# Staged first loads, first sums strip by strip, and output halves at the end of a two-layer LoRA kernel

## The chip, the cores and the metric

The kernel runs on one core of a Trainium2 chip. The metric is device time in microseconds of one execution; lower is better. The core has five engines that each work through their own instruction queue in program order: TensorE (PE; its weight loads are a row of their own, PEld), VectorE (DVE), ScalarE (ACT), GpSimd (POOL), and SyncE (SP), which here only issues DMAs. POOL issues the gathers (indirect DMAs). An instruction that waits holds up everything behind it on its engine.

## The reference

Two residual LoRA layers over x (64 requests of 64 tokens, 1024 channels, fp32), one after the other:

```python
x = x + _L0_cond_ref(x, L0_cond_A, L0_cond_B, itok_B_4_50)
#   Bx = x @ B[id].T ; out = Bx @ A[id].T       one adapter of rank 16 per request
x = x + _L1_cond_ref(x, itok_B_0_7, L1_cond_W, L1_cond_Wr, L1_cond_A, L1_cond_B)
#   base = x @ W.T
#   logits = x @ Wr.T + 5 * one_hot(language id)   8 experts, the top 2, softmax of the two
#   lora = sum over experts of gate * (x @ A[e].T) @ B[e].T
#   out = base + 2 * lora
```

## The kernel before

x is held transposed (channels on the partitions) in 8 blocks of 512 tokens. A block is two tiles of 1 MB, `("x", k, 0)` and `("x", k, 1)`, with 4 chunks of 128 channels each; a strip of a tile is 128 tokens of it. Block k goes through two phases. The first, `early(k)`, is layer 0:

- `gather` fetches the rows of B (tile gb) and of A (tile ga) of the block's 8 requests from HBM, 512 KB each, by an indirect DMA on POOL.
- `turn` transposes gb on PE (tile pt), 4 chunks at a time, and ACT copies it out (tile bt).
- `project` multiplies bt by all 8 chunks of x into one PSUM tile (the pb with 128x128 outputs, 64 instructions), and DVE masks it to bx.
- `adapt` multiplies ga by bx, one half of the channels at a time (tile px), and DVE adds the result to x, one strip of one half at a time: 8 sums a block.

The second phase, `late(k)`, is the routing part of layer 1: `rows` multiplies each strip of x by A and Wr of layer 1 (tiles ph; the two operands lie side by side in a1_sb, whose last columns POOL copies from wr_c), `gates` works out the gates on DVE, `weigh` transposes the gated rows on PE (pg). A strip of `rows` needs the sums of both halves of that strip.

The base product x @ W.T, with the identity added to W's diagonal blocks (`add_identity`, DVE) for the residual, is done for two blocks at a time with a two-level Strassen scheme of 7 outer products, in the order 1, 2, 6, 7, 5, 3, 4; each has 7 inner products numbered likewise (`step(n, k)`), and the last two inner products of each outer one are put off and interleaved with the next. The very first outer product is done directly (`whole_product`, tile pw). `leave` adds a PSUM result to the outputs on DVE, `done` stores a finished output tile (512 KB). For the first pair the sums of weights are made on POOL and kept in HBM; later pairs load them back.

No order of instructions is written by hand. Each step is put into a `Plan` with its engine and an assumed duration, what it reads and writes, an urgency `at` (lower is earlier), and kb for a DMA's size. `Plan.order` simulates the engines with these durations, takes at each point the most urgent step that can start within 0.2 us of the earliest, and the program is issued in the order of the simulated starts. What an instruction really waits for is added afterwards from the tiles that it touches. The assumed numbers therefore decide only the order in each queue. LAG is the assumed hand-over between engines, LAND and KB the landing and rate of a DMA, GATHER the extra time of a gather, SET the time at which an engine is free at the beginning.

What touches the change, by lines: `add` 57, `order` 64, `consts` 308, `load` 353, `gather` 367, `turn` 379, `project` 400, `adapt` 428, `gates` 504, `load_w` 597, `add_identity` 606, `products` 777 with `done` 892 and `step` 940. Every instruction is recorded through one helper, so the profile calls them all L29; they are told apart by the tiles. The beginning is set up by these lines (988 to 997):

```python
    consts()
    for k, at in ((0, -58), (1, -42)):
        for i in range(2):
            load(k, i, at)
        gather(k, "gb", b0, at - 1)
        gather(k, "ga", a0, at)
    ...
            load_w(q0[0] + i, q0[1] + j, at)
    early(0, -40)
```

In the program before, SP's queue begins with the ids of layer 0, both halves of block 0, wr_c, the language ids (ids1_sb), A of layer 1, four tiles of W, both halves of block 1, and the other twelve tiles of W. POOL's begins with the gathers gb and ga of block 0, gb and ga of block 1, the copy of wr_c into a1_sb, and then gb of block 2 and so on, as their two buffers come free.

Of the kernel before, what the change touches and what calls it, by code (L numbers as in the profile page):

```python
# [14 lines left out]
P = 128  # L15
# [18 lines left out]
class Plan:  # L34
# [8 lines left out]

    LAG = 0.3
    LOOK = 0.2
    LAND = 2.2
    KB = 350.0
    GATHER = 4.0
    AHEAD = 6.0
    PACE = {"DVE": 0.4, "POOL": 0.75}  # L50
    SET = {"SP": 1.2, "DVE": 3.1, "POOL": 3.6}

# [3 lines left out]

    def add(self, eng, fn, reads=(), writes=(), at=0.0, take=(), kb=0, sb=False):

        self.steps.append(
            dict(n=len(self.steps), eng=eng, fn=fn, reads=list(reads), writes=list(writes),  # L60
                 at=at, take=list(take), kb=kb, sb=sb)
        )

    def order(self):
        steps = self.steps
        wrote, read, users, tag_of, turns = {}, {}, {}, {}, {}
        for st in steps:
            n, dep = st["n"], set()
            for k in st["reads"]:
                dep.update(wrote.get(k, ()))  # L70
            for k in st["writes"]:
                dep.update(wrote.get(k, ()))
                dep.update(read.get(k, ()))
            for k in st["reads"]:
                read.setdefault(k, []).append(n)
            for k in st["writes"]:
                wrote[k], read[k] = [n], []
            for tag, tile_ in st["take"]:
                tag_of[tile_] = tag
                turns.setdefault(tag, []).append(n)  # L80
            for k in st["reads"] + st["writes"]:
                users.setdefault(k[0], set()).add(n)
            dep.discard(n)
            st["dep"] = dep
        held = [[] for _ in steps]
        left, last = {}, {}
# [5 lines left out]
        for st in steps:  # L92
            for d in st["dep"]:
                after[d].append(st["n"])
        needs = [len(st["dep"]) for st in steps]
        ready = {st["n"] for st in steps if not st["dep"]}
        free = {tag: [0.0] * c for tag, c in self.slots.items()}
# [8 lines left out]
        def start(n, e):  # L106
            st = steps[n]
            t = clock.get(e, 0.0)
            if st["kb"] and e == "SP":
                t = max(t, moved - self.AHEAD)  # L110
            for d in st["dep"]:
                t = max(t, end[d] + (0.0 if where[d] == e and not steps[d]["kb"] else self.LAG))
# [65 lines left out]
def kernel(  # L178
# [129 lines left out]
    def consts():  # L308
# [3 lines left out]
            [], [("ids1",)], -53, kb=32,  # L312
        )
        plan.add({"SP": 0.4}, lambda e: sp.dma_start(a1_sb[:, :, :P], a1), [], [("a1",)], -45, kb=512)
        plan.add({"SP": 0.4}, lambda e: sp.dma_start(b1_sb, b1), [], [("b1",)], -29, kb=512)

        def spread(e):
            pool.tensor_copy(a1_sb[:, :, P:], wr_c)

        def languages(e):  # L320
            per = P // SEQ
# [15 lines left out]

        plan.add({"POOL": 0.3}, spread, [("wr_c",)], [("wr",)], -45)
        plan.add({"DVE": 1.0}, languages, [("ids1",)], [("bias",)], -45)


# [11 lines left out]
    def load(k, i, at):  # L353
        t = ("x", k, i)

        def fn(e):
            made[t] = new("q", [P, HC, TB], f"x_{k}_{i}")
            sp.dma_start(
                made[t],
                xT[i * HC * P : (i + 1) * HC * P, k * TB : (k + 1) * TB].rearrange(  # L360
                    "(c p) t -> p c t", p=P
                ),
            )

        plan.add({"SP": 0.5}, fn, [], part(t), at, [("q", t)], kb=1024)

    def gather(k, tag, table, at):
        def fn(e):
            made[tag, k] = new(tag, [P, D], f"{tag}_{k}")
            pool.indirect_dma_start(  # L370
                out=made[tag, k],
                out_offset=None,
                in_=table,
                in_offset=bass.IndirectOffsetOnAxis(ap=idx[:, k : k + 1], axis=0),
            )

        plan.add({"POOL": 1.1}, fn, [], [((tag, k),)], at, [(tag, (tag, k))], kb=512)

    def turn(k, g, at):
# [11 lines left out]
        def out(e):  # L391
            act.copy(made[bt][:, g * PER : (g + 1) * PER, :], made[pt])

        plan.add(
            {"PE": 0.65}, fn, [(("gb", k),)] + [(bt, 0)] * g, [(pt,)] + [(bt, 0)] * (g == 0), at,
            [("l", pt)] + [("bt", bt)] * (g == 0),
# [3 lines left out]
    def project(k, at):  # L400

        pb, bx = ("pb", k), ("bx", k)

        def fn(e):
            made[pb] = new("l", [P, GT], f"pb_{k}")
            made[bx] = new("bx", [P, GT], f"bx_{k}")
            for c in range(NC):
                for gi in range(NG):
# [10 lines left out]
        def out(e):  # L419
            dve.tensor_tensor(made[bx], made[pb], mask, ALU.mult)  # L420

        plan.add(
            {"PE": 2.2}, fn, [(("bt", k), 1), (("bt", k), 2)] + whole(k), [(pb,), (bx,)], at,
            [("l", pb), ("bx", bx)],
        )
        plan.add({"DVE": 0.3}, out, [(pb,)], [(bx,)], at - 8)

    def adapt(k, h, at):
# [22 lines left out]
        def out(gi):  # L451
# [6 lines left out]
        plan.add(  # L458
            {"PE": 1.4}, fn, [(("ga", k),), (("bx", k),)], [(t,) for t in px], at,
            list(zip(tags, px)),  # L460
        )
        for gi in range(NG):
            xs = part(x, gs=[gi])
            plan.add({"DVE": 0.7}, out(gi), [(px[gi],)] + xs, xs, at - 2)

    def rows(k, at):
# [3 lines left out]
        def strip(j):  # L470
# [14 lines left out]
            def out(e):  # L485
# [5 lines left out]
            plan.add(  # L491
                {"PE": 1.92}, fn, [("a1",), ("wr",)] + xs, [(ph,)], at + j,
                [("l", ph)] * (j % 2 == 0),
# [10 lines left out]
    def gates(k, at):  # L504
# [51 lines left out]
        plan.add({"DVE": 0.9}, lambda e: first(e, 1), [(sm, 1)], [(sm, 2)], at, sb=True)  # L556
        plan.add({"DVE": 0.7}, second, [(sm, 2)], [(sm, 3)], at)
        plan.add({"ACT": 0.25}, exp, [(sm, 3)], [(sm, 4)], at)
        plan.add({"DVE": 0.9}, lambda e: first(e, 2), [(sm, 3)], [(sm, 5)], at, sb=True)
        plan.add({"DVE": 0.8}, share, [(sm, 4)], [(sm, 6)], at, sb=True)  # L560
        plan.add({"DVE": 0.6}, weights, [(sm, 5), (sm, 6)], [(sm, 7)], at, sb=True)
        plan.add({"DVE": 0.7}, gated, [(sm, 7), (h, 0), (h, 1)], [(h, 0), (h, 1)], at, sb=True)

    def weigh(k, at):
# [9 lines left out]
        def out(e):  # L574
            act.copy(made[hg], made[pg].rearrange("p j t -> p (j t)"))

        plan.add(
            {"PE": 0.5}, fn, [(h, 0), (h, 1)], [(pg,), (hg,)], at, [("l", pg), ("hg", hg)]
        )
# [17 lines left out]
    def load_w(i, j, at):  # L597
# [5 lines left out]

        plan.add({"SP": 0.4}, fn, [], [(t,)], at, [("s", t)], kb=256)

    def add_identity(i, at):
# [7 lines left out]

        plan.add({"DVE": 0.5}, fn, [(t,), (("bx", 0),)], [(t,)], at, sb=True)

# [18 lines left out]

    DVE = {"DVE": 0.7}
    POOL = {"POOL": 1.3}

# [115 lines left out]
    def gate_sum(s, n, hd, at):  # L754
# [9 lines left out]
        if n != 3:  # L764
            plan.add({"DVE": 0.42}, fn, [(h,)], [(d,)], at, [("hd", d)], sb=True)
        hd[n] = {
# [10 lines left out]
    def products(s):  # L777
# [24 lines left out]
        ALL = (0, 1)  # L802

        def whole_product(n, i, c):

# [18 lines left out]
            if oh is not None:  # L824
                reads += [("b1",), (whole_h[n],)]
            plan.add(
                {"PE": 3.45 + 0.87 * (oh is not None)}, fn, reads, [(ps,)], at(), [(tag, ps)]
            )
# [4 lines left out]
        def product(n, ps, k, start):  # L833
            last = hd[n][k] if n in (2, 3, 7, 4) and k in (2, 3, 7, 4) else None
            sw, (tx, tk) = wt[n][k], ti[n][k]
# [3 lines left out]
            def fn(e):  # L839
# [3 lines left out]
                for j in range(QC):  # L843
                    mm = [(made[sw][:, c, j * P : (j + 1) * P], tx()[:, c]) for c in range(QC)]
                    if last is not None:
                        o = (oh * 2 + row) * QC + j
                        mm.append((b1_sb[:, o * P : (o + 1) * P], last[0]()))
                    for c, (lhs, rhs) in enumerate(mm):
# [9 lines left out]

            reads = [(sw,)] + tk + ([("b1",), last[1]] if last is not None else [])
            plan.add(  # L860
                {"PE": 1.75 + 0.87 * (last is not None)}, fn, reads, [(ps,)], at(),
                [("a" if k == 1 else "b", ps)] * start,
# [29 lines left out]
        def done(n, i, cs, js):  # L892
# [14 lines left out]
            if oh is None:  # L907
                return
            left[n, i] = left.get((n, i), 2) - 1
            if left[n, i] == 0:  # L910
                o0 = (oh * 2 + i) * QO

# [27 lines left out]
        def step(n, k):  # L940
            i, j = {1: (0, 0), 2: (0, 0), 6: (1, 0), 7: (1, 1), 5: (1, 1), 3: (0, 1), 4: (1, 0)}[k]
            if k in (1, 6, 5, 3):
                ps = ("pa", s, n)
                product(n, ps, k, k == 1)
                leave(n, ps, i, ALL, (j,))
                if k == 5:
                    leave(n, ("pb2", s, n), 1, ALL, (1,), True)
# [3 lines left out]
            else:  # L951
                product(n, ("pb2", s, n), k, k == 7)
                if k == 4:
                    leave(n, ("pb2", s, n), 1, ALL, (0,), True)
# [7 lines left out]
        for n in ORDER:  # L962
# [20 lines left out]
            step(n, 5)  # L983
            rest = [(n, 3), (n, 4)]
        for k in rest:
            step(*k)

    consts()
    for k, at in ((0, -58), (1, -42)):
        for i in range(2):  # L990
            load(k, i, at)
        gather(k, "gb", b0, at - 1)
        gather(k, "ga", a0, at)
    for q0, at in (((0, 0), -43), ((0, 2), -39), ((2, 0), -37), ((2, 2), -36)):
        for i, j in ((0, 0), (1, 0), (1, 1), (0, 1)):
            load_w(q0[0] + i, q0[1] + j, at)
    early(0, -40)
    for i in range(4):
        add_identity(i, -30)
# [73 lines left out]
```

## Time and profile before

| what | us |
|---|---|
| median of three runs (lowest, highest) | 527.1 (525.8, 527.23) |
| the profiled execution's own time | 525.91 |
| its span, first to last instruction | 524.1 |
| PE busy, PEld busy | 504.3, 439.6 |
| DVE, POOL, ACT busy | 294.0, 167.7, 41.1 |
| gathers gb and ga of block 0, issue to landing | 7.6, 7.9 |
| a_sb (A of layer 1) and ids1_sb, issue to landing | 14.7, 13.0 |

The span and the execution's own time differ by 1.8 us, which lies around the span. In the timeline and the page a line reads: line, engine, operation, the tile written and the tiles read, shape, count, then busy time and the mean of one, and in the last column the engine's idle time just before and what ended it. One fp32 matmul shows as two instructions. The clock granted to TensorE was 0.998 of full speed over the span.

### The profile page before, as it was taken

The numbers are of one execution on the slowest core, as the hardware profiler recorded it, in microseconds if no ns is written. First come the engines' busy times: TensorE is split into PE (matmuls) and PEld (weight loads), VectorE is DVE, ScalarE is ACT, GpSimd is POOL, SyncE is SP. The second block draws the span as 40 slices with busy tenths as digits, with TensorE's granted clock in tenths as the row PEclk, the third lists the DMA queues.
The fourth block names the chain that finished last, engine by engine and source line by source line (L and its number), as shares of the span: only waits on it lengthen the run. The fifth ranks groups of instructions, "written<-read, shape, count | busy, mean of one in ns | idle before, by whom it ended". The sixth has DMA issues, their size and how long they took to land.

```text
span 524.1 us, 8532 instructions
## 1 busy us (share of the span) xinstructions
PE 504.3 (96%) x3432; PEld 439.6 (84%) x3432; DVE 294.0 (56%) x572; ACT 41.1 (8%) x81; POOL 167.7 (32%) x139
## 2 busy tenths in 40 slices
PE   1799999999999999999999999999999999999995
PEld 1657988889888988898888998889888898888884
DVE  0679997987974273616674255435476417433632
ACT  1111010001000100012000100001200010001000
POOL 3180068091323144123234313312332323433200
PEclk9999999999999999999999999999999999999999
DMA  8999346689666249726566436844546623710222
GB/s 289 361 362 399 141 147 244 235 298 351 214 220 216 65 141 340 252 73 202 174 204 206 161 100 208 280 138 145 160 155 194 210 84 105 217 41 0 81 80 80
DMA packets 53687, 99.19 MB, mean 189 GB/s; under 512 B 4880, under 2 KB 10000, under 8 KB 53648
## 3 DMA queue, kind: packets, MB, share of 16 engines
q1 hardware_dynamic: 51344, 90.26, 51.8%
q0 software_dynamic: 2304, 8.39, 4.5%
q8 instruction: 27, 0.44, 0.3%
q14 instruction: 12, 0.10, 0.0%
HBM read 69.01 MB, written 29.62 MB: 188 GB/s over the span
## 4 chain that ended last, share of the span: by engine, by line
PE 95%; DMA 2%; DVE 1%; issue 0%; SPq 0%
PE pa L29 39%; PE pb L29 37%; PE ph L29 11%; PE px L29 3%; PE pw L29 3%; DMA ids_sb<-in_ids 2%; PE pt L29 1%; PE pg L29 1%; SPq L29 0%; DVE o L29 0%; DVE bias L29 0%; DVE lang L29 0%; DVE bx L29 0%
## 5 line engine op out<-in xcount | busy, mean ns | idle before, releaser
L29 PE MATMUL pa<-ti,s 128*128 128x256 f32 x432 | 102.5, 381 | 0.0
L29 PE MATMUL pb<-ti,s 128*128 128x256 f32 x384 | 95.7, 380 | 0.0
L29 PEld LDWEIGHTS pa<-ti,s 128*128 128x128 f32 x432 | 80.7, 190 | 11.2 <-issue 0.2
L29 PEld LDWEIGHTS pb<-ti,s 128*128 128x128 f32 x384 | 72.2, 190 | 10.0 <-POOL s L29 0.2
L29 PEld LDWEIGHTS ph<-a_sb,x 128*128 128x128 f32 x512 | 62.7, 190 | 3.3 <-issue 2.2
L29 PE MATMUL ph<-a_sb,x 128*128 128x136 f32 x512 | 63.3, 279 | 2.0 <-issue 2.0
L29 POOL TENSOR_TENSOR ti<-x,ti 128x512 f32<-128x512 f32 x24 | 30.9, 1288 | 78.8 <-PE pb L29 77.9
L29 DVE TENSOR_TENSOR o<-pb,o 128x512 f32<-128x512 f32 x48 | 33.1, 690 | 34.3 <-PE pb L29 20.8
L29 PE MATMUL pa<-x,s 128*128 128x256 f32 x216 | 52.0, 380 | 0.0
L29 POOL TENSOR_TENSOR ti<-t,ti 128x512 f32<-128x512 f32 x18 | 25.2, 1400 | 71.9 <-PE pb L29 54.8
L29 POOL TENSOR_TENSOR ti<-x 128x512 f32<-128x512 f32 x24 | 30.5, 1270 | 52.0 <-PE pb L29 35.9
L29 PEld LDWEIGHTS pa<-x,s 128*128 128x128 f32 x216 | 40.1, 190 | 5.2
L29 DVE TENSOR_TENSOR x<-px,x 128x512 f32<-128x512 f32 x64 | 39.8, 682 | 8.0 <-POOL ti L29 4.3
L29 PE MATMUL pa<-t,s 128*128 128x256 f32 x168 | 41.1, 381 | 0.8 <-DVE o L29 0.8
L29 POOL TENSOR_TENSOR ti<-t 128x512 f32<-128x512 f32 x18 | 24.4, 1353 | 43.4 <-PE pb L29 33.9
L29 DVE TENSOR_TENSOR o<-pa,u 128x512 f32<-128x512 f32 x32 | 22.1, 690 | 26.1 <-PE pa L29 24.8
L29 PEld LDWEIGHTS pa<-t,s 128*128 128x128 f32 x168 | 31.5, 190 | 5.7 <-DVE o L29 1.2
L29 DVE TENSOR_TENSOR u<-pb,u 128x512 f32<-128x512 f32 x21 | 14.5, 690 | 25.6 <-ACT u L29 20.7
L29 PE MATMUL pb<-hg,b_sb 128*128 128x256 f32 x96 | 28.5, 379 | 0.0
L29 DVE TENSOR_TENSOR o<-pa,v 128x512 f32<-128x512 f32 x16 | 11.0, 690 | 26.1 <-PE pa L29 25.8
L29 DVE TENSOR_TENSOR v<-pa,u 128x512 f32<-128x512 f32 x16 | 11.0, 689 | 24.4 <-PE pa L29 24.4
L29 PE MATMUL pb<-x,s 128*128 128x256 f32 x96 | 23.9, 381 | 0.0
(109 smaller groups left out, 592.8 us busy)
## 6 DMA issues: line engine op xcount, KB each, us to landing
s<-s_kept SPq DMA_DIRECT2D x147, 256.0 KB, 2.7
x<-in_xT SPq DMA_DIRECT2D x16, 1024.0 KB, 6.2
out_T<-o SPq DMA_DIRECT2D x32, 512.0 KB, 3.1
s_kept<-s SPq DMA_DIRECT2D x28, 256.0 KB, 3.8
s_kept<-w SPq DMA_DIRECT2D x18, 256.0 KB, 5.1
w<-in_w SPq DMA_DIRECT2D x16, 256.0 KB, 10.1
s_kept<-m SPq DMA_DIRECT2D x3, 256.0 KB, 5.1
a_sb<-in_a SPq DMA_DIRECT2D x1, 512.0 KB, 14.7
```

Of the source, the lines that this page charges most:

```text
L29: return self._tc.keep_in_program_order(f(*args, **kwargs))
```

## The change

The diff does five things. (1) The first x tile is loaded in two DMAs of 512 KB. (2) Some early DMAs are held back by a data dependency: a copy of one column on POOL, from the tile that has to land first into the tile that is to be loaded next, so that the next load waits for POOL and POOL for the first load. The second half of block 0 is so held by the first half of ("x",0,0), and A of layer 1 by gb of block 0. The new argument `behind` asks the planner alone to place a step after another has begun; it adds no wait of its own. (3) DVE's sums of block 0 get urgencies that go by strip; the biases of the language ids and the identity of W are to follow all of block 0's sums (`whole(0)`); `project` is planned as two halves. (4) In the last outer product of the last pair the inner products 4 and 3 change places, the shared PSUM result of product 7 is added to the output before product 5 is done, and the output tiles are stored in halves of 256 KB. (5) The planner's durations are changed.

```diff
-    LAG = 0.3
+    LAG = 0.2
-    LAND = 2.2
+    LAND = 1.8
-    GATHER = 4.0
+    GATHER = 1.5
-    PACE = {"DVE": 0.4, "POOL": 0.75}
-    SET = {"SP": 1.2, "DVE": 3.1, "POOL": 3.6}
+    PACE = {"DVE": 0.36, "POOL": 0.73}
+    SET = {"SP": 1.2, "DVE": 3.1, "POOL": 2.9}
...
+            st["begun"] = {d for k in st["behind"] for d in wrote.get(k, ())} - dep
...
+            for d in st["begun"]:
+                t = max(t, steps[d]["start"] + 0.1)
...
+        def hold(e):
+            pool.tensor_copy(a1_sb[:, 0, :1], made["gb", 0][:, :1])
+        plan.add({"POOL": 0.2}, hold, [(("gb", 0),)], [("a1",)], -56)
         plan.add({"SP": 0.4}, lambda e: sp.dma_start(a1_sb[:, :, :P], a1), [], [("a1",)], -45, kb=512)
-        plan.add({"SP": 0.4}, lambda e: sp.dma_start(b1_sb, b1), [], [("b1",)], -29, kb=512)
+        plan.add({"SP": 0.4}, lambda e: sp.dma_start(b1_sb, b1), [], [("b1",)], -29, kb=512, behind=[("a1",)])
...
-        plan.add({"DVE": 1.0}, languages, [("ids1",)], [("bias",)], -45)
+        plan.add({"DVE": 1.0}, languages, [("ids1",)] + whole(0), [("bias",)], -45)
...
+        held = (k, i) == (0, 1)
+        def hold(e):
             made[t] = new("q", [P, HC, TB], f"x_{k}_{i}")
+            pool.tensor_copy(made[t][:, 0, :1], made["x", 0, 0][:, 0, :1])
+        cuts = ((0, HC // 2), (HC // 2, HC)) if (k, i) == (0, 0) else ((0, HC),)
...
+        if held:
+            plan.add({"POOL": 0.2}, hold, part(("x", 0, 0), [0]), part(t), at, [("q", t)])
+        for c0, c1 in cuts:
+            plan.add(
+                {"SP": 0.5}, lambda e, c0=c0, c1=c1: fn(c0, c1),
+                [], part(t, range(c0, c1)), at, [("q", t)] * (not held and c0 == 0),
+                kb=256 * (c1 - c0), behind=[("a1",)] * (k == 1) + [(t, 0, 0)] * (c0 > 0),
+            )
...
-        plan.add({"POOL": 1.1}, fn, [], [((tag, k),)], at, [(tag, (tag, k))], kb=512)
+        plan.add(
+            {"POOL": 1.1}, fn, [], [((tag, k),)], at, [(tag, (tag, k))], kb=512,
+            behind=[(("x", 0, 1), 0, 0)] * ((tag, k) == ("ga", 0)) + [("a1",)] * (k == 1) + [(("px", 1, 1, 0),)] * (k > 1),
+        )
...
-            {"PE": 2.2}, fn, [(("bt", k), 1), (("bt", k), 2)] + whole(k), [(pb,), (bx,)], at,
+        for h in range(2):
+                {"PE": 0.94}, lambda e, h=h: fn(range(h * HC, (h + 1) * HC)),
+                [(("bt", k), 1), (("bt", k), 2)] + part(("x", k, h)), [(pb,)] + [(bx,)] * (1 - h),
+                at + 0.1 * h, [("l", pb), ("bx", bx)] * (1 - h),
...
-            plan.add({"DVE": 0.7}, out(gi), [(px[gi],)] + xs, xs, at - 2)
+            plan.add({"DVE": 0.62}, out(gi), [(px[gi],)] + xs, xs, at - 2 + 1.5 * gi * (k == 0))
...
-        plan.add({"SP": 0.4}, fn, [], [(t,)], at, [("s", t)], kb=256)
+        plan.add({"SP": 0.4}, fn, [], [(t,)], at, [("s", t)], kb=256, behind=[("a1",)])
...
-        plan.add({"DVE": 0.5}, fn, [(t,), (("bx", 0),)], [(t,)], at, sb=True)
+        plan.add({"DVE": 0.5}, fn, [(t,)] + whole(0), [(t,)], at, sb=True)
...
+            if last(n):
+                def half(e):
+                    t0 = k * TB + js[0] * HT
+                    sp.dma_start(
+                        outT[o0 : o0 + QO, t0 : t0 + HT].rearrange("(c p) t -> p c t", p=P),
+                        q(n, i, ALL, js),
+                    )
+                plan.add({"SP": 0.1}, half, qk(n, i, ALL, js), [], at() + 2, kb=256)
+                return
...
-                leave(n, ps, i, ALL, (j,))
-                if k == 5:
+                leave(n, ps, i, ALL, (j,), k == 5 and last(n))
+                if k == 5 and not last(n):
                     leave(n, ("pb2", s, n), 1, ALL, (1,), True)
...
+                if k == 7 and last(n):
+                    leave(n, ("pb2", s, n), 1, ALL, (1,))
...
-            rest = [(n, 3), (n, 4)]
+            rest = [(n, 4), (n, 3)] if last(n) else [(n, 3), (n, 4)]
...
-    consts()
-    for k, at in ((0, -58), (1, -42)):
-        for i in range(2):
-            load(k, i, at)
+    for k, at in ((0, -60), (1, -42)):
+        load(k, 0, at)
         gather(k, "gb", b0, at - 1)
+        load(k, 1, at)
         gather(k, "ga", a0, at)
+        if k == 0:
+            consts()
     for q0, at in (((0, 0), -43), ((0, 2), -39), ((2, 0), -37), ((2, 2), -36)):
-        for i, j in ((0, 0), (1, 0), (1, 1), (0, 1)):
-            load_w(q0[0] + i, q0[1] + j, at)
+        for i, j in ((0, 0), (0, 1), (1, 0), (1, 1)):
+            load_w(q0[0] + i, q0[1] + j, at + 2 * i * (at == -43))
```

Left out are the steps' other planned durations, each lowered by some hundredths to tenths of a microsecond (a turn from 0.65 to 0.44, a DVE sum from 0.7 to 0.62, a POOL sum from 1.3 to 1.25, an adapt from 1.4 to 1.1).

## The prediction

> **What bounds the kernel now.** I read the page's first part, then its chain of waits, then PE's waits, then the timeline of the first 30 and the last 20 us.
>
> ```profile
> PE 504.3 (96%) x3432; PEld 439.6 (84%) x3432; DVE 294.0 (56%) x572; ACT 41.1 (8%) x81; POOL 167.7 (32%) x139
> PE 95%; DMA 2%; DVE 1%; issue 0%; SPq 0%
> PE pt L29 <- DMA gb<-in_b,idx: 10.6, 1, 10.6
> PE ph L29 <- issue: 2.0, 1, 2.0
> PE px L29 <- DVE bx L29: 1.6, 1, 1.6
> PE pa L29 <- DVE o L29: 0.8, 1, 0.8
> ```
>
> PE is idle for only 524.1 - 504.3 = 19.8 us. The four waits are 15.0 of these; the other 4.8 lie between PE's last product and the end of the span. Between 21.3 and 513 us PE never stops. The change takes no product away, so all that it can win lies in these 19.8 us, and all that it can lose is a new hole in the full stretch. The beginning:
>
> ```profile
> 10.65 1.94 PE L29 MATMUL pt<-ident,gb 128*128 128x128 f32 x8 [10.65 <-DMA gb<-in_b,idx]
> 12.51 2.51 PE L29 MATMUL pb<-x,bt 128*32 128x128 f32 x64
> 14.96 0.66 PE L29 MATMUL pt<-ident,gb 128*128 128x128 f32 x4
> 15.78 0.36 DVE L29 TENSOR_SCALAR lang<-ids_sb 64x32 f32<-64x32 int32 x2 [12.90 <-DMA ids_sb<-in_ids]
> 16.85 0.28 DVE L29 TENSOR_TENSOR bx<-pb,mask 128x128 f32<-128x128 f32 x1
> 17.19 2.07 PE L29 MATMUL px<-bx,ga 32*128 32x128 f32 x64 [1.57 <-DVE bx L29]
> 18.87 0.49 DVE L29 TENSOR_TENSOR w<-w,ident 128x128 f32<-128x128 f32 x2 [1.74 <-DMA w<-in_w]
> 19.28 4.87 DVE L29 TENSOR_TENSOR x<-px,x 128x512 f32<-128x512 f32 x8
> 21.26 3.94 PE L29 MATMUL ph<-a_sb,x 128*128 128x136 f32 x32 [2.01 <-issue]
> ```
>
> Three things delay the first ph. gb lands at 10.5. The product pb is over at about 15.0, yet bx comes at 16.85, because DVE stands at lang, whose ids (32 KB) took 13.0 us to land. The first sum waits behind the identity, which waits for a tile of W. All three are one cause: everything was issued at once and shares the DMA engines. The windows view gives about 400 GB/s from 4 us on, and 1.1 MB moved by 6 us, while 3.1 MB of x and gathers for block 0, 2.1 MB of gathers for blocks 1 to 3, and W were in line by 26 us.
>
> The end:
>
> ```profile
> 513.09 0.69 DVE L29 TENSOR_TENSOR o<-pa,v 128x512 f32<-128x512 f32 x1 [3.62 <-PE pa L29]
> 513.82 0.69 DVE L29 TENSOR_TENSOR o<-pb,o 128x512 f32<-128x512 f32 x1
> 513.84 1.13 PE L29 MATMUL pa<-t,s 128*128 128x256 f32 x4 [0.78 <-DVE o L29]
> 519.32 0.69 DVE L29 TENSOR_TENSOR o<-pb,o 128x512 f32<-128x512 f32 x1 [1.90 <-PE pb L29]
> out_T<-o SPq DMA_DIRECT2D x1, 512.0 KB, 2.8
> ```
>
> Product 3 writes the PSUM tile that DVE is still reading from product 5. After the last sum (over at 520.0) a 512 KB store takes 2.8 us to land.
>
> **Beginning, step by step.** I follow the first ph, since PE is full from there on.
>
> 1. First half of ("x",0,0). The whole tile, issued at 1.19, landed 5.7 later, at 6.9; its 1.05 MB had passed by 5.9, so landing trails the last byte by 1.0. Half of it has passed at 4.55: landed at 5.5. POOL, which has issued gb (2.89 to 4.0) and stands idle, copies the column (0.23, the row of the a_sb copy) by 5.8; SP issues ("x",0,1) at 5.9, its bytes following about 0.9 later.
> 2. gb. Ahead of or beside it now lie 1.05 MB of x and 0.06 of small loads, with its own 0.52: 1.64 MB, passed at 4.55 + 1.12/0.4 = 7.3, landed at **8.2**. Gathers elsewhere in the trace took 4.0 with little beside them, 7.6 here: bounds 6.9 and 10.5. I take 8.2, as the queue is half as long.
> 3. pt at 8.3; from pt to pb it was 1.86 before, so the first half of pb runs from 10.1 to 11.4 (half of 2.51).
> 4. ("x",0,1) and ga together are 1.57 MB from 7.3 on: passed by 11.2, landed by 12.2. Alone, the tile would land at 10.9; with gb of block 1 and A of layer 1 taking 0.5 MB before it, at 13.5. I take **12.3**, later than the 11.5 of before (9.8 after an issue at 1.7): this is what staging costs. ga was issued at 4.3, and comes behind the copy at about 6; it lands by 12 and is needed at 14.
> 5. Second half of pb 12.3 to 13.6, bx and hand-overs 0.5 (at 45 us bx follows pb by 0.15; px followed bx by 0.34): px at 14.1 instead of 17.19. The lang and bias steps (1.1 us) and the identity now follow the sums. There DVE had 2.7 us idle before the gates, which hides them; without that cover they would delay the gates by up to 1.1, not PE.
> 6. First sum 1.3 after px starts (47.22 to 48.53 in block 1): 15.4. By strips, ph needs one sum of each half; the second half's px is over at 16.2, its sum at 16.9, so ph starts at **17.2**. A of layer 1 is issued behind gb, at 8.5, queues behind ("x",0,1), and lands at 13.5 to 15.3: in time, but next in line to be late.
>
> 21.26 - 17.2 = **4.1 us**. Before, half of the transposes of block 1 (0.44 for 4) lay in a PE hole, at 14.96. Now gb of block 1 goes behind the A hold on POOL and lands at about 14; the hole between px and ph (16.2 to 17.2) can take 0.4 to 0.9 of them. Nothing gained or lost, bounds -0.4 and +0.4.
>
> What is queued behind the two holds? On POOL ga, both gathers of block 1 and the wr_c copy (all treated above); on SP, behind A, block 1's x and all W. W's first tiles then land at about 17.5 and are needed at 25 (pw was 7.9 after ph); block 1's x lands near 23, needed at 39. In exchange 1.57 MB of gathers for blocks 2 and 3, issued at 13.7, 19.6 and 25.9 before (first used at 69), are planned later: W should be complete some 4 us earlier than before, when it landed at 39 to 40 and DVE waited for it twice (0.53, 0.43).
>
> **The two rules.** The Trainium skill's page "DMA: Bandwidth & Descriptors", section Bandwidth, tells one to batch DMAs to 1 MiB or more and fits a DMA as 2.0 us plus its bytes at 436 GB/s. Taken one after another, two halves of 512 KB would then cost 6.4 us against 4.4: 2.0 lost. The row speaks otherwise: W's 256 KB loads, queued twelve deep, ran at 350 to 377 GB/s from 30 to 40 us, so the fixed part overlaps; I count nothing for the cut. For the last store, where nothing overlaps, rule and row both count: below. The page "TensorE: Matmul & The Clock Gate", Part 1, says that the array runs at half clock until about 3.4 us of sustained work. An earlier start with holes (11.4 to 12.3, 13.6 to 14.1) may keep it cold through px: up to 2.1 us more. The granted clock shows 1.00 there, but pb took 2.51 at the start against 1.9 later, so something is slow early on; px, after a 1.6 us hole, took 2.07, hardly more than the 2 x 1.1 of block 1. I take the row: none.
>
> **End.** Product 4 comes first and uses the PSUM tile that was emptied after product 7, so the 0.78 goes; DVE's sum of product 5 (0.69) is over before product 3 needs its tile 2.6 us later. The last store is 256 KB: the 512 KB were moved at 385 GB/s in some 1.3 us, half of that is 0.65; the median 256 KB load took 2.7, which would save 0.1. The store is the nearer row: 0.5. Together **1.3 us**.
>
> **The full stretch.** 17 to 110 us is where DVE is dense: 22.7 busy of 24 between 40 and 64 us. Its inputs (gates behind ph, W behind the DMAs, sums behind px) all move by about 4 us with PE, and PE had no wait there, so I count no hole; bounds 0 and 4. Later DVE is at 53% (207 of 390). The planner's lower durations match what one sees (0.61 from sum to sum, 1.23 for POOL alone), so its order need not be worse.
>
> Sum: 4.1 + 1.3 = **5.4 us**. The profiled execution took 525.91; less 5.4 is 520.5. The median of the runs is 1.2 above it, which would give 521.7. I forecast **521.5**.
>
> **Rivals.** A measurement here tells a change from none at about 0.3%, 1.6 us.
>
> - *Given back* (0.16): PE reaches DVE's dense stretch 4 us early and waits there for the sums of block 1 or the t tiles. For: DVE's 95% between 40 and 64. Against: those sums' own inputs come earlier too, and DVE's waits for W go. It leaves the end's 1.3 and a little: 525.
> - *All of it* (0.11): x gets the larger share of the DMA engines, ("x",0,1) lands at 11, ph starts at 15.9 and both transposes of block 1 are hidden: 1.3 + 0.4 more, 519.8. Against: before, that tile got only about half the rate while the gathers ran.
> - *The hold changes nothing for gb* (within the forecast): gb still lands at 10.5. Then pb is over at 15.0, bx and px follow at once (15.5), ph at 18.6: DVE's new order alone gives 2.7, with the end 4.0: 523.
> - *Slower* (0.07): the order is frozen with a gather assumed to land 4.4 us after its start (1.1 + 1.5 + 1.8), where loaded ones took 7.3 to 9.8. A gather for which PE's transposes are queued too early then stops PE by 3 to 5 us. It decides from two such stalls on, once they pass the 5.4; two of 4 us make 529.5. Against: gb of later blocks was issued long before its use (25.9 for use at 69), and only block 1's is near.
>
> The chances: forecast 0.66, all 0.11, given back 0.16, slower 0.07. Faster by over 0.3%: 0.66 + 0.11 + 0.10 (the better part of given back) = 0.87; within 0.06; slower 0.07. Forecast's own bounds are 519.9 to 523.5; the range runs from 519.4, below "all", to 524.8, taking in much of "given back".
>
> **What would show it.** In the changed profile: pt released by gb at 8 to 8.5; no lang before bx; ph near 17.2 with a PE wait before it under 1.2; no PE wait on DVE o at the end, the last store 256 KB landing in 2.3; PE busy still 504, waits between 20 and 500 us near zero. Wrong if gb lands after 10, if A or ("x",0,1) lands after 15, or if PE waits appear between 25 and 110.

## The result

| | before | changed |
|---|---|---|
| median of six runs (lowest, highest), us | 526.98 (525.34, 527.23) | 521.72 (521.31, 522.09) |
| profiled execution's own time, its span | 525.91, 524.1 | 521.59, 519.8 |
| ratio to before, 95% interval | | 0.9914 (0.9899 to 0.9929) |

The change makes the kernel 0.9% faster; 521.5 was forecast. The first line of the changed kernel's page, then PE's waits in it from the view of who waited for whom (total us, times, longest):

```profile
PE 504.9 (97%) x3432; PEld 439.3 (85%) x3432; DVE 300.9 (58%) x572; ACT 41.1 (8%) x81; POOL 170.0 (33%) x141
```

```profile
PE pt L29 <- DMA gb<-in_b,idx: 9.7, 1, 9.7
PE pb L29 <- DMA x<-in_xT: 0.6, 1, 0.6
PE px L29 <- DVE bx L29: 0.4, 1, 0.4
PE ph L29 <- issue: 0.2, 1, 0.2
```

Idle time on PE up to the first ph is 10.9 us instead of 14.2, the wait on DVE at the end is gone, and no wait has come in between 19 and 515 us. The beginning in the timeline, the lines of PE and POOL that answer to those of before:

```profile
4.58 0.18 POOL L29 COPY x<-x 128x1 f32<-128x1 f32 x1 [0.58 <-DMA x<-in_xT]
9.64 0.18 POOL L29 COPY a_sb<-gb 128x1 f32<-128x1 f32 x1 [2.95 <-DMA gb<-in_b,idx]
9.72 1.94 PE L29 MATMUL pt<-ident,gb 128*128 128x128 f32 x8 [9.72 <-DMA gb<-in_b,idx]
11.59 1.54 PE L29 MATMUL pb<-x,bt 128*32 128x128 f32 x32
13.72 1.08 PE L29 MATMUL pb<-x,bt 128*32 128x128 f32 x32 [0.59 <-DMA x<-in_xT]
15.20 2.07 PE L29 MATMUL px<-bx,ga 32*128 32x128 f32 x64 [0.40 <-DVE bx L29]
16.45 4.88 DVE L29 TENSOR_TENSOR x<-px,x 128x512 f32<-128x512 f32 x8 [1.30 <-PE px L29]
17.20 1.25 PE L29 MATMUL pt<-ident,gb 128*128 128x128 f32 x8
18.64 7.65 PE L29 MATMUL ph<-a_sb,x 128*128 128x136 f32 x64 [0.19 <-issue]
```

The two copies are the holds. gb lands at 9.6, the second x tile at 13.6. Nothing stands before bx on DVE; all of block 1's transposes (x8) fit between px and ph. The first ph starts at 18.64 instead of 21.26. The end:

```profile
513.22 0.69 DVE L29 TENSOR_TENSOR o<-pb,o 128x512 f32<-128x512 f32 x1 [1.90 <-PE pb L29]
515.81 0.69 DVE L29 TENSOR_TENSOR o<-pa,v 128x512 f32<-128x512 f32 x1 [1.90 <-PE pa L29]
```

From PE's last product, where this last sum starts, to the end of the span it is 519.8 - 515.8 = 4.0 us; before it was 4.8.

One thing the first profile didn't tell shows in the many runs of the kernel before that were taken beside the experiments: its times lie in two groups, 525.0 to 526.3 and 526.9 to 528.1, about half in each. The changed kernel has one group, 521.2 to 522.1 in twelve runs. The profile of before (525.91) comes from the lower group, so its span tells of a 4.3 us gain where the medians tell of 5.3.

### The profile page after: what moved, and what is told of

Its sections match the earlier page's. It is cut to its first block, busy times and chain, and to the rows that moved or that the text cites. A ratio compares the mean times of both kernels' runs of the same rounds, so it can differ in the third digit from the quotient of the medians.

```text
span 519.8 us, 8542 instructions
## 1 busy us (share of the span) xinstructions
PE 504.9 (97%) x3432; PEld 439.3 (85%) x3432; DVE 300.9 (58%) x572; ACT 41.1 (8%) x81; POOL 170.0 (33%) x141
## 4 chain that ended last, share of the span: by engine, by line
PE 96%; DMA 2%; DVE 0%; issue 0%; SPq 0%; POOL 0%
PE pa L29 39%; PE pb L29 38%; PE ph L29 11%; PE px L29 3%; PE pw L29 3%; DMA x<-in_xT 2%; PE pt L29 1%; PE pg L29 1%; DVE o L29 0%; SPq L29 0%; DVE bx L29 0%; POOL x L29 0%
## 5 line engine op out<-in xcount | busy, mean ns | idle before, releaser
L29 POOL TENSOR_TENSOR ti<-x,ti 128x512 f32<-128x512 f32 x24 | 32.2, 1340 | 78.0 <-PE pb L29 77.1
L29 DVE TENSOR_TENSOR u<-pb,u 128x512 f32<-128x512 f32 x21 | 14.5, 689 | 25.1 <-ACT u L29 20.7
L29 POOL TENSOR_TENSOR s<-w,w 128x512 f32<-128x512 f32 x12 | 17.0, 1418 | 36.0 <-DVE w L29 36.0
```

Of the source, the lines that this page charges most:

```text
L29: return self._tc.keep_in_program_order(f(*args, **kwargs))
```

## The experiments

Twelve kernels, one of them the changed one again; of three only one execution was timed. "First ph" is the point from which PE is full; the kernel before has it at 21.3, the changed one at 18.6.

**The changed kernel again**, as measure for the others: median 521.63, gb 9.2, second x tile 13.2, first ph 18.2. So single profiles of the beginning differ by 0.4.

> The changed kernel once more, as the measure for the others of this call. Its times lay between 521.3 and 522.1 with one level, where those of the kernel before lie in two groups (525.0 to 526.4 and 526.9 to 528.1). Expected: median 521.5 to 521.9, one level, gb landed at 9.5 to 9.7, second x tile at 13.4 to 13.8, first ph at 18.6. If the first loads vary from one execution to the next, first ph lies elsewhere by more than 0.5.

**The hold of the second x tile, taken away.**

```diff
-        held = (k, i) == (0, 1)
+        held = False
-            behind=[(("x", 0, 1), 0, 0)] * ((tag, k) == ("ga", 0)) + [("a1",)] * (k == 1) + [(("px", 1, 1, 0),)] * (k > 1),
+            behind=[] + [("a1",)] * (k == 1) + [(("px", 1, 1, 0),)] * (k > 1),
```

> The changed kernel without the hold of the second x tile by the first half of the first: SP issues it at once, and ga follows gb on POOL without a wait; the hold of A stays. If the hold is what brings gb forward: gb lands at 10.4 to 10.6 as before the change, the second x tile by 9.5, px about 15.4, first ph at 18.3 to 18.8. If the hold costs more than it brings (the second x tile is what px waited for in the changed kernel): first ph earlier than 18.4.

```profile
11.97 1.94 PE L29 MATMUL pt<-ident,gb 128*128 128x128 f32 x8 [11.97 <-DMA gb<-in_b,idx]
21.15 7.65 PE L29 MATMUL ph<-a_sb,x 128*128 128x136 f32 x64 [0.25 <-issue]
```

gb lands at 11.9, later than in any other run, and the first ph is back at 21.2; the one execution took 524.1. In the changed kernel the hold is thus worth 2.5 us: what it does is to give the gather the DMA engines. The held tile pays for it, as it lands at 13.6 instead of 11.0. The 2.5 are not what the staging gains on the kernel before, since without the hold gb lands even later than there (10.5).

**DVE's order alone, on the kernel before** (biases and identity behind the sums, sums by strip).

```diff
-        plan.add({"DVE": 1.0}, languages, [("ids1",)], [("bias",)], -45)
+        bias_fn.append(languages)
...
+    plan.add({"DVE": 1.0}, bias_fn[0], [("ids1",)] + whole(0), [("bias",)], -45)
-            plan.add({"DVE": 0.7}, out(gi), [(px[gi],)] + xs, xs, at - 2)
+            plan.add({"DVE": 0.7}, out(gi), [(px[gi],)] + xs, xs, at - 2 + 1.5 * gi * (k == 0))
-        plan.add({"DVE": 0.5}, fn, [(t,), (("bx", 0),)], [(t,)], at, sb=True)
+        plan.add({"DVE": 0.5}, fn, [(t,)] + whole(0), [(t,)], at, sb=True)
```

> The kernel before, with DVE's order alone changed (biases and identity behind all sums of block 0, sums by strip). By the prediction's working: gb still at 10.5, pb over at 15.0, px at 15.5, first ph at 18.6 unless A of layer 1 (landed at 18.1 before) or its last columns are later; time 2.7 below the kernel before, 524.3. If the DMA queue and not DVE's order was what held the beginning: first ph above 20 and less than 1 us gained.

```profile
19.38 3.94 PE L29 MATMUL ph<-a_sb,x 128*128 128x136 f32 x32 [1.11 <-DVE x L29]
31.68 1.36 PE L29 MATMUL pb<-x,bt 128*32 128x128 f32 x32 [2.92 <-DMA x<-in_xT]
32.96 5.07 PE L29 MATMUL pw<-x,w 128*128 128x512 f32 x8
```

The first ph comes at 19.4, a gain of 1.9; the staging of the changed kernel adds 0.7 to that (1.2 in its second profile). Yet the median is 528.34, ratio 1.0017 (1.0000 to 1.0033), where 524.3 was expected. The second line says where the gain goes in this execution: the planner now puts block 1's pb ahead of pw, and block 1's x, which shares the DMA engines with everything else, isn't there. Behind this hole the granted clock is 0.50 for 3.4 us (from 32.3 on), and the first eight instructions of pw take 5.07 instead of the 3.70 of the changed kernel:

```profile
33.00:34.00 1.00, 1.00 (x5) 0.48 (x3) 0.82 (x5) 0.00 (x0) 0.07 (x1) 0.50 1.06 341
```

(The columns are named below, under the small loads; the 0.50 is the clock.) But the profiled execution, 529.48, is the slowest of 20. The times lie in two groups here too: 7 from 525.0 to 525.7 and 13 from 527.5 to 529.5. The lower one is 0.4 below the lower group of the kernel before; as its middle is 3.7 below that of the upper, more than the half rate's 1.7, its wait for x is probably shorter, but none of it was profiled. In the changed kernel the same pb starts at 26.2 without a wait.

**The last stores whole again** (`if last(n)` around `half` becomes `if False`).

> The changed kernel with the last four output stores whole again (two of 512 KB in place of four of 256 KB); product 4 still before 3. Read from the profile: no PE wait on DVE o at the end, as in the changed kernel; from PE's last product to the end of the span 4.6 to 4.8 us as before the change, against 4.0 in the changed kernel. If the order and not the halves shortened the end: 4.0 here too.

No wait on DVE o at the end; PE's last sum starts at 515.86 and the span ends at 520.6: 4.7 us. So the order of the last products took the 0.78 and the halves took 0.7 to 0.8.

**The old durations** in the changed kernel (LAG 0.3, LAND 2.2, GATHER 4.0 and the steps' own).

> The changed kernel planned with the durations of the kernel before (LAG, LAND, GATHER, PACE, SET and the steps'), all else as changed. SP's and POOL's first instructions stay in the same order. If the durations matter to the order in the full stretch: PE waits of some us appear between 25 and 500 us, time 523 or more. If they don't: 521.3 to 522.2.

Median 524.11, ratio 0.9954 (0.9936 to 0.9972). Nothing but assumed numbers differs, but PE gets a new wait in the full stretch (the lines of DVE and PE on it):

```profile
28.42 0.49 DVE L29 TENSOR_TENSOR w<-w,ident 128x128 f32<-128x128 f32 x2 [2.69 <-DMA w<-in_w]
34.40 0.28 DVE L29 TENSOR_TENSOR bx<-pb,mask 128x128 f32<-128x128 f32 x1
34.73 1.17 PE L29 MATMUL px<-bx,ga 32*128 32x128 f32 x32 [1.91 <-DVE bx L29]
```

The medians are 2.4 us apart, the spans of the two profiled executions 3.2. Of these 1.9 are this wait, and 0.9 the second half of pb at half rate in this execution (below). The durations decide no wait, only an order. PE's order at this place is that of the changed kernel; in DVE's queue an identity now stands ahead of the gates and of bx and waits 2.69 for its tile of W, so that bx comes at 34.4 instead of 28.4.

**The small loads.** The DMA engines of the changed kernel have a hole just where gb should land. Columns of the windows view: the window, its length, PE, PEld, DVE, ACT, POOL busy, granted clock, share of the DMA engines, GB/s.

```profile
4.00:5.00 1.00, 0.00 (x0) 0.00 (x0) 0.00 (x0) 0.00 (x0) 0.26 (x2) 1.00 1.05 408
5.00:6.00 1.00, 0.00 (x0) 0.00 (x0) 0.00 (x0) 0.00 (x0) 0.89 (x1) 1.00 0.74 156
6.00:7.00 1.00, 0.00 (x0) 0.00 (x0) 0.00 (x0) 0.00 (x0) 0.24 (x1) 1.00 0.45 80
7.00:8.00 1.00, 0.00 (x0) 0.00 (x0) 0.00 (x0) 0.00 (x0) 0.00 (x0) 1.00 0.77 248
8.00:9.00 1.00, 0.00 (x0) 0.00 (x0) 0.00 (x0) 0.00 (x0) 0.00 (x0) 1.00 0.96 383
```

```profile
DMA packets 76, 0.08 MB, mean 80 GB/s; under 512 B 60, under 2 KB 60, under 8 KB 76
q1 hardware_dynamic: 60, 0.01, 5.6%
```

The second fence is the DMA view of 6 to 7 us: all 60 packets of SP's queue (q1) are under 512 B. These are wr_c and the language ids, which SP issues between the two x tiles. I put both, and then the ids alone, behind A of layer 1:

```diff
-        plan.add({"SP": 0.4}, lambda e: sp.dma_start(wr_c, wr), [], [("wr_c",)], -53, kb=8)
+        plan.add({"SP": 0.4}, lambda e: sp.dma_start(wr_c, wr), [], [("wr_c",)], -44.6, kb=8, behind=[("a1",)])
...
-            [], [("ids1",)], -53, kb=32,
+            [], [("ids1",)], -44.5, kb=32, behind=[("a1",)],
```

> The changed kernel, with the two small loads (wr_c and the language ids, 32 KB each) issued behind A of layer 1 in place of between the two x tiles of block 0. Theory S (the small loads' 256 B pieces stand in SP's queue ahead of the second x tile and are what leaves the DMA engines half idle from 5.2 to 8 us): DMA at about 400 GB/s from 3 us on, gb lands at 8.2 to 8.6 (9.6 in the changed kernel), the second x tile at about 12.2 (13.6), first ph at 17.0 to 17.5 (18.6), time 520.3, 1.4 below the changed kernel's 521.7. Theory G (the gather's own start is slow, and the second x tile starts late because of its hold): gb still at 9.4 to 9.7, first ph not before 18.2, time within 0.4 of 521.7.

> Only the language ids are issued late; wr_c stays between the x tiles. If the ids are the slow one of the two (a broadcast: 128 reads of one 256 B row), this has the whole effect of moving both: gb at 8.2 to 8.6, first ph near 17.3. If the count of small pieces decides, half of the hole stays: first ph near 18. Theory G: first ph 18.6 as in the changed kernel.

Both late:

```profile
8.16 1.94 PE L29 MATMUL pt<-ident,gb 128*128 128x128 f32 x8 [8.16 <-DMA gb<-in_b,idx]
14.58 1.94 PE L29 MATMUL pb<-x,bt 128*32 128x128 f32 x32 [2.62 <-DMA x<-in_xT]
16.92 3.80 PE L29 MATMUL px<-bx,ga 32*128 32x128 f32 x64 [0.40 <-DVE bx L29]
22.16 7.65 PE L29 MATMUL ph<-a_sb,x 128*128 128x136 f32 x64 [0.34 <-issue]
```

Theory S was right on gb and wrong on the time. gb lands at 8.0; with the ids alone moved, at 7.5, so it is the ids that slow it. But the kernel gets slower than the changed one: median 525.14, ratio to before 0.9976 (0.9966 to 0.9986), where 520.3 was expected; with the ids alone the one execution took 526.73. The second x tile lands at 14.5 (16.0 there), not earlier. And the second half of pb takes 1.94 instead of 1.08, px 3.80 instead of 2.07: PE works at half rate. I call it theory C that the array does so until it has been busy for some microseconds, and again after a hole. The 3.5 us by which the first ph is later are 0.9 of x tile, 0.9 of pb and 1.7 of px.

**A later third stage** (on the kernel with the small loads late): A no longer held by gb but issued right behind the second x tile, the gathers of block 1 held until that tile has landed.

```diff
-        plan.add({"POOL": 0.2}, hold, [(("gb", 0),)], [("a1",)], -56)
...
+        held = (tag, k) == ("gb", 1)
+        def hold(e):
+            made[tag, k] = new(tag, [P, D], f"{tag}_{k}")
+            pool.tensor_copy(made[tag, k][:, :1], made["x", 0, 1][:, 0, :1])
...
```

> The kernel with the small loads late, and the third stage hung up differently: A of layer 1 is no longer held by gb but simply follows the second x tile in SP's queue, and the gathers of block 1 are held until the second x tile has landed. Theory Q (the second x tile landed at 14.5 in the kernel with the small loads late because gb, landing early, let A and block 1's gathers loose beside it): it lands at 11.5 to 12.3, pb's second half follows the first with less than 0.5 us of a hole, first ph at 17 to 17.5, or 18.7 if the array is still at half rate for px; time 520.2 to 522. If the x tile is late for a reason of its own: it lands after 13.5 again, px at half rate, time 524 to 525.

> The same with 28 transposes of the identity ahead on PE until about 7 us. Theory C: pt 1.1 instead of 1.94, px 2.07 whatever the holes, first ph at or below 17.2, time 520 or less, one level. If half rate plays no part: the same time as without them within 0.4.

Medians 524.03, ratio 0.9954 (0.9937 to 0.9970), and 524.16, ratio 0.9957 (0.9940 to 0.9974). Both are slower than the changed kernel. The second x tile lands at 13.6 in both although block 1's gathers no longer run beside it, so theory Q fails as far as the gathers go. A was issued at 5.4 here, 0.4 after the tile, where the changed kernel issues it at 9.9; what a tile with neither beside it would do was not tried. In the first, gb of block 1 now comes too late: PE waits 1.46 for it at 24.1. The 28 transposes ahead in the second helped pt (1.09 for 1.94), but then PE was idle from 9.9 to 13.7 and fell back to half rate. Here the granted clock shows it, in the first of the two, after a hole of 2.3 us:

```profile
14.00:15.00 1.00, 0.78 (x30) 0.51 (x20) 0.17 (x1) 0.00 (x0) 0.63 (x1) 0.99 0.90 232
15.00:16.00 1.00, 0.82 (x15) 0.82 (x18) 0.12 (x1) 0.00 (x0) 0.70 (x2) 0.50 1.06 230
17.00:18.00 1.00, 1.00 (x28) 1.00 (x24) 0.65 (x2) 0.00 (x0) 0.00 (x0) 0.50 1.02 381
18.00:19.00 1.00, 1.00 (x22) 0.88 (x19) 0.79 (x3) 0.00 (x0) 0.00 (x0) 0.81 1.05 354
```

**Half rate and the two groups of the kernel before.** Its holes on PE are 1.6 us ahead of px and 2.0 ahead of ph. First I put 44 transposes of the identity at PE's start, then instead 11 into the first hole and 8 into the second; the other queues stay as they are. The second edit (FIRST is 1, the half of `adapt` that comes first; the last four lines are in `rows`):

```diff
+            if (k, h) == (0, FIRST):
+                for i in range(11):
+                    pe.transpose(made[px[0]][:, i % HC, :], ident, ident)
...
+                if (k, j) == (0, 0):
+                    fill = new("a", [P, QC, HT], "fill")
+                    for i in range(8):
+                        pe.transpose(fill[:, 0, :P], ident, ident)
```

> The kernel before with 44 transposes of the identity put ahead on PE, from 1.6 us until gb lands, their result read by nobody; every queue is otherwise in the same order. Theory C (the array runs at half rate until it has been busy for some us, and in the slower group of the kernel before px falls into that time, 1.7 us): pt of block 0 takes 1.1 instead of 1.94, pb 1.9 instead of 2.51, all executions in one group near 524.5 to 525.5, none above 526.5. If the two groups come from the DMAs (when a tile or a gather lands): the two groups stay, 1.5 to 2 us apart, and the median moves by less than 1.

> The kernel before with its two early holes on PE filled: 11 transposes of the identity queued ahead of px and 8 ahead of the first ph, results read by nobody; every queue is otherwise in the same order and no wait is moved. Theory C (in the slower group the array has fallen to half rate in these holes and the first ph strips run at half rate, 1.7 us): the slower group vanishes, all executions between 525.2 and 526.2, median some 1 us below the kernel before. If the groups come from the DMAs or from something else: the two groups stay, 525.4 and 527.2.

The first misses: median 527.86, ratio 1.0018 (1.0006 to 1.0031). pt and pb do run at full rate (1.09 and 1.95), but bx still waits for the language ids, so the holes grow to 2.1 and 2.6, and then the clock falls:

```profile
21.48 5.61 PE L29 MATMUL ph<-a_sb,x 128*128 128x136 f32 x32 [2.62 <-issue]
```

```profile
22.00:23.00 1.00, 1.00 (x9) 1.00 (x8) 1.00 (x2) 0.00 (x0) 0.00 (x0) 0.81 1.04 385
23.00:24.00 1.00, 1.00 (x7) 1.00 (x6) 1.00 (x3) 0.00 (x0) 0.00 (x0) 0.50 1.07 399
```

The first ph strips take 5.61 instead of 3.94: 1.7 more, the distance of the two groups. With the holes filled, 22 executions lie between 525.27 and 526.22, while of the 29 of the kernel before beside them 14 lie above 526.9. Its first ph starts at 21.24, no earlier than before; the second group just is gone (ratio 0.9985, 0.9977 to 0.9993). So the two groups come from what happens on PE in these two holes, and the half rate has the right size for it.

No execution of the slower group of the kernel before was itself profiled, but the mean granted clock of each is on record. Of 102 executions of it beside the experiments, the 50 of the lower group (mean 525.6) have 0.997 to 1.000; of the 52 of the upper (mean 527.3) one has 0.997 and the rest 0.994 or 0.995. Half rate for 3.4 us lowers the mean over 524 us by 0.003. (The 0.998 of the profiled execution is a fall after PE's last product, at 522.3.)

The clock's entries in the traces also tell when it falls. In all 14 traces the changes of one trace lie whole multiples of 3.41 us apart, while the first lies elsewhere each time: at 13.7 in the kernel before, at 12.6 and 13.3 in the two profiles of the changed one. Ahead of the first there is no entry, which is why the view reads 1.00 there; up to there products take almost twice their time (until 20.9 with the small loads late). In the 3.41 us before each of the five falls in a beginning PE had been idle for 1.9, 2.3, 2.3, 2.8 and 3.4 us. After stretches with 1.8 or less of idle, such as one of 1.5 in the kernel before, no trace shows a fall; after 1.98, at the end of the changed kernel, none came either. The holes of the kernel before, 1.6 and 2.0 with 2.1 of px between them, can put at most 2.0 into one such stretch. So it lies at the edge, and where the stretches happen to lie would decide the group. This last step is an inference, as no run moved them.

**An attempt at a better version**: small loads late, the first x tile cut after one chunk, 28 transposes at the start and 14 between the halves of pb.

> An attempt at a better version: small loads late, the first x tile cut after one chunk of four in place of two (the second x tile then issued at about 4.2), A held by gb as in the changed kernel, 28 transposes of the identity ahead on PE and 14 between the halves of pb so that the array stays at full rate. Expected: gb lands at 8 to 8.5, the second x tile at 12.5 to 13.5, px 2.07 at full rate, first ph at 17 to 18, time 520.6 to 521.4. If the second x tile lands at 14 or later as in the kernel with the small loads late alone: first ph at 18.7, 522 or more.

```profile
15.34 2.07 PE L29 MATMUL px<-bx,ga 32*128 32x128 f32 x64 [0.41 <-DVE bx L29]
19.45 7.68 PE L29 MATMUL ph<-a_sb,x 128*128 128x136 f32 x64 [0.86 <-POOL a_sb L29]
```

px runs at full rate and starts as in the changed kernel; then ph waits for a_sb's last columns, since wr_c now lands late. The transposes at the start end 1.90 us before gb lands, and the clock falls once more, from 8.8 to 12.2, so that pt takes 1.78, not 1.09:

```profile
9.00:10.00 1.00, 1.00 (x7) 0.95 (x5) 0.00 (x0) 0.46 (x1) 0.89 (x1) 0.50 1.09 416
```

Median 522.28, ratio 0.9921 (0.9903 to 0.9938), where 520.6 to 521.4 was expected: no better. No version measured beats the changed kernel.

## Why the prediction was right, and where not

The changed kernel's profiled execution took 521.59; from the profile of before I had worked out 520.5. By terms, predicted and measured:

| term | predicted | measured |
|---|---|---|
| first half of the first x tile lands | 5.5 | 4.5 |
| gb lands | 8.2 | 9.6 |
| second x tile lands | 12.3 | 13.6 |
| first ph | 17.2 | 18.6 |
| gain to the first ph | 4.1 | 2.6 |
| block 1's transposes hidden | 0 (bounds 0.4) | 0.4 |
| end | 1.3 | 1.6 |
| full stretch | 0 | -0.3 |

The last row is what is left of the spans' 4.3 us after the other gains.

- **The mechanism of the beginning** was right: gb, lang, and the identity were the three delays; the last two are gone, and gb comes 0.9 earlier. Without the hold the first ph is back at 21.2; DVE's order alone gives 1.9 of the 2.6. From pb's end to the first ph the working agrees to 0.2: 13.6 to 17.2 predicted, 14.8 to 18.6 measured.
- **The mis-sized term** is step 2: "0.06 of small loads" were counted by their bytes, 0.15 us. They left the DMA engines half idle for about 2 us. From the landing of the half tile to that of gb the working has 2.7 us; it took 5.1, with both small loads moved away 3.2, with the ids alone moved 2.7. The x tile is 1.3 later than reckoned; that stage is late for a reason that stays open.
- **The clock rule** (the Trainium skill's page "TensorE: Matmul & The Clock Gate", Part 1) was weighed and set aside on the row of px (2.07). In the changed kernel that holds for px, which takes 2.07 again; with the small loads late it takes 3.80, as the rule would have it. But the row came from the lower group; about half of the executions before took some 1.7 us more, which is what the half rate costs. So part of the gain, 1.0 to 1.4 us of the medians' 5.3 (the distance of the median of before from its profile, or from the middle of its lower group), is that group's disappearance, which no term of mine contains.
- **Luck.** The sum put the profiled execution at 520.5, 1.1 too low. From there I moved up by 1.0 to 521.5, for the distance between the profile and the median of before, without knowing what it was. In the changed kernel, with its one group, that distance is 0.1 (521.59 and 521.72). Two errors of a microsecond cancelled, so that 521.5 is nearer to the median than the working deserves.
- **Rule on small DMAs.** For the cut of the x tile nothing was lost: its halves land at 4.5 and 5.9, the whole tile before at 6.9. The fit of 2.0 us plus bytes that the prediction worked with stands in another section of the Trainium skill's page "DMA: Bandwidth & Descriptors", "Anatomy of one DMA — SWDGE (gpsimd) path", for DMAs issued by GpSimd; these are SP's. The last 512 KB store of the kernel before took 2.8, where the fit gives an estimate of 3.2. For the last store I took 0.5 between 0.1 and 0.65; 0.7 to 0.8 was measured, above the bound.
- **The rivals.** *Given back* did not happen in the changed kernel: no PE wait in the dense stretch, with DVE as full as before (22.69 of 24 us from 40 to 64). PE waits in the full stretch when the parts come alone: with DVE's order alone for block 1's x (until 31.7), with the old durations for its bx (until 34.7). The durations, to which the working gave nothing, are thus worth 2.4 us by the medians. *The hold changes nothing for gb*: in the changed kernel it is worth 2.3 us for gb. DVE's order alone I had put at 2.7; it brings the first ph forward by 1.9, and the median not at all. *Slower*: PE waits for no gather after the first.
- **Open:** why the second x tile lands 8.0 to 9.0 us after its issue in most runs, 9.4 with the small loads late and 10.9 with the ids alone late; the working had 6.4.

## What to carry to other kernels

When everything is issued at once, the load that is needed first shares the DMA engines with all others. Here one hold made the later load land 2.6 us later and the earlier one 2.3 us earlier, and that paid because PE waited for the earlier one. Don't count small loads by their bytes alone; but moving them away helped only the gather here, and the kernel got slower. In a program ordered by a planner, test the assumed durations like any other part. And when a kernel's times lie in two groups, compare their granted clocks and look for holes of about 2 us on PE: a hole of 2.3 to 2.9 us cost another 1.5 to 1.7 us behind it.

## What was unexpected of the hardware

- Holes of 1.9 to 3.8 us on PE were followed by a granted clock of 0.50 that lasted 3.4 us (after 1.9, 2.3, 2.6 and 2.9) and 6.8 us (after 3.8), once and twice the window of about 3.4 us that the Trainium skill's page "TensorE: Matmul & The Clock Gate", Part 1, gives. The page has the clock fall after an idle window of that length; here 1.9 to 2.8 us of idle within 3.41 were enough. After holes of 0.2 to 0.6 it was not seen, nor in the profile of before after 1.6 and 2.0. The half rate before PE's first warm-up shows in the durations (px 3.80 instead of 2.07) while the granted clock reads 1.00.
- Two loads of 32 KB, in pieces under 512 B, took the DMA engines from 408 to 80 GB/s for about two microseconds, and held up a gather on the other queue by 1.6 (landed at 9.6; 8.0 with both moved away).
